# A four-layer decoder on one core: keys of the cross attentions ahead of the query, wide products of ones in every attention, and reordered slot arithmetic in the two routed layers

## The chip, the core and the metric

The kernel is one program for one core of one Trainium2 chip. The time is the device time of one execution in microseconds (us). Three runs of the kernel before took 962.3, 957.73 and 956.75 us; their median is 957.73. One further execution was recorded by the hardware profiler: it took 954.99 us, and the durations below are from it. The engines are called PE (TensorE matmuls), DVE (VectorE), ACT (ScalarE), POOL (GpSimd) and SP (SyncE, which here only issues transfers).

## The reference

The input `x` is 16 sequences of 64 tokens with 128 channels, float32, so 1024 tokens. A second input `ctx_1024` of the same shape is the context of the cross attentions. Each of four layers has an attention, a cross attention and a feed-forward part; each of the twelve is added to its input and normalised:

```python
x = _layernorm(x + _L0_attn_ref(x, ...), axis=-1)
x = _layernorm(x + _L0_xattn_ref(ctx_1024, x, ctx_1024, ...), axis=-1)
x = _layernorm(x + _L0_ffn_ref(x, ...), axis=-1)
...
x = _layernorm(x + _L3_ffn_ref(x, ...), axis=-1)
```

The cross attentions, here that of layer 1, take the query from `x`, and keys and values from the context; those of layers 0, 2 and 3 differ in masks, scale and the number of heads:

```python
q = _split_heads(Q @ Wq + bq)
k = _split_heads(K @ Wk + bk)
v = _split_heads(V @ Wv + bv)
scores = jnp.einsum('bhqd,bhkd->bhqk', q, k) / np.sqrt(HEAD_DIM)
attn = jax.nn.softmax(scores, axis=-1)
out = jnp.einsum('bhqk,bhkd->bhqd', attn, v)
...
return out @ Wo + bo
```

The feed-forward part of layer 2 sends each token to the best of 16 experts (a switch) and adds a shared expert; that of layer 3 takes the best two of 8 experts:

```python
_, top_idx = jax.lax.top_k(logits, TOP_K)          # layer 2, TOP_K = 1
...
masked_inputs = scores.T[:, :, None] * x[None, :, :]
gate_up = jnp.einsum('eth,ehf->etf', masked_inputs, gate_up_proj)
gate, up = jnp.split(gate_up, 2, axis=-1)
expert_out = jnp.einsum('etf,efh->eth', up * jax.nn.silu(gate), down_proj)
shared = jax.nn.silu(x @ w_gate.T) * (x @ w_up.T) @ w_down.T
...
topk_logits, topk_idx = jax.lax.top_k(logits, TOP_K)   # layer 3, TOP_K = 2
w = jax.nn.softmax(topk_logits, axis=-1)
...
h = jax.nn.gelu(jnp.einsum('th,ehi->tei', xt, W1) + b1, approximate=False)
y = jnp.einsum('te,teh->th', gates, jnp.einsum('tei,eih->teh', h, W2) + b2)
```

## The kernel before

**Names.** A tag stands for a sublayer: `xa0` to `xa3` are the cross attentions of layers 0 to 3, `at1` and `at3` the self attentions of layers 1 and 3, `lb` the two layers of local attention in layer 0, `sf` a feed-forward part with given experts (layer 1), `rc` the recurrence of layer 2, `sw` the switch layer (2), `tt` the top-2 layer (3).

**Two halves.** The tokens are cut into two halves of 512, h = 0 and 1. Each half is a Python generator that goes through its sublayers. `side_by_side` advances the two in turns, half 0 with a lead of 5 turns in `first_stream` (xa0, lb, at1, xa1, sf, rc, xa2, the router's scores) and of 2 in `second_stream` (at3, xa3, scores). A `yield` is thus the place where the other half's instructions are put in between. A scheduler then orders the instructions of each engine, and an engine works through its own list strictly in that order. The switch layer stands between the two streams, and the top-2 layer behind the second.

**An attention** (L400 on) first projects the query q from x (L424, L426) and then the keys: a matmul and a copy on ACT give k, and POOL multiplies it with the mask of one head group after the other to give the masked keys km (L436, four pieces of 128x512 with heads of 8 channels, eight in xa2 with heads of 4). Values v follow. Then the work goes in four steps of 64-wide blocks (eight in xa2): `weights` makes the scores in psum (L475, 16 matmuls per tile and step), takes their maximum and subtracts it on DVE (L519, L520) and the exponential on ACT (L523). `turn` transposes e on PE (L535, 2 x 4 per step) and copies it to eT on ACT (L538). `weigh` multiplies eT with the values (L556, 32 matmuls). `gather` and the projection at the end give `po`, `y` is the sum with the input, and `close` (L195 to L203) makes the statistics on DVE, the inverse deviation rstd on POOL (L198 an addition, L201 a power) and the normalised xt on DVE. `flip` transposes xt on PE (`px`) and so makes the x of the next sublayer. `steps` of the two halves alternate; the loop has a `yield` after each, and one ahead of `flip`.

**Products of ones.** `keep_busy` (L156) is a matmul of a 128x128 matrix of ones with itself, spread to 512 columns, in bf16, whose result the next matmuls into the same psum tile overwrite. It stands ahead of each projection of q and k, ahead of the unmasked scores (two per step), and, where the flag `spare` is set (L532), ahead of the transposes (two per step). `spare` is set in xa0, at3 and xa3, not in at1, xa1 and xa2. Where the scores have a mask (xa0, xa2, xa3), two matmuls of 128x512 in bf16 add it (L486).

**Relative positions.** at3 writes its relative scores to DRAM (`at_mem`) and reads them back (`at_rel`), all on SP's queue.

**The routed layers** do the expert work on 23 tiles of 128 slots. `choose` gives the one-hot choice `hots`; for the two best, weights `tt_w` come from ACT and POOL. `place` (L1192 to L1310) finds the slot of each token: `every` is the sum of the choices, `pp` the running counts on PE, `nt` the count per expert rounded up to 128, `end` and `begin` its running sums, `sf` the slot, `in_tile` and `at_row` one-hot forms of its tile and row, and `pid` a sum of 16 or 32 matmuls that gives the token of every slot; `ids` are those as integers (a free slot reads a row of zeros). `whose` and `owner` tell the expert of each tile. `tiles_in_step` gathers the rows of the tiles (`got`, on POOL's queue, six ahead), transposes them, and calls `first`, `flip` and `second` for the two layers of the expert; it also calls `between(k)` once for each tile, from k = -1.

In the switch layer the slots are gathered back at the end (`sw_back`, eight gathers on POOL's queue) and added to the shared expert's result (L1436). The shared expert of half 0 is computed at the end of half 0's stream, that of half 1 inside the switch layer: `share_up` for its two chunks f, with `between` putting the rest at tiles 0, 2 and 4.

In the top-2 layer the results are scattered to rows of `tt_out` given by `tt_outs` (on POOL's queue), and read back as `tt_back` on SP, one row of 512 bytes per partition and descriptor. The weights and the output rows of the slots come from a second sum of 16 matmuls, `tt_pw`, which the code before makes from `tt_wof` right behind `place`.

**Loads.** `load_switch_down` loads the second weights of the 16 experts ahead of the switch layer, `load_top2` (L1613) all weights of the 8 experts of the top-2 layer, 4 MB in four transfers on SP, called right behind the switch layer. `mask_zero` (L706) loads the integer mask of xa3 and turns it into additions.

Of the kernel before, what the change touches and what calls it, by code (L numbers as in the profile page):

```python
# [11 lines left out]
F32 = mybir.dt.float32  # L12
# [25 lines left out]
class Kernel:  # L38
    def __init__(self, ctx, tc, dram, where):
# [9 lines left out]
        self.xt = []  # L49
# [135 lines left out]
    def close(self, pool, h, y, tag, shift=False):  # L185
# [10 lines left out]
        for i in range(4):  # L196
            nc.vector.bn_aggr(mv[:, i, :], stats[:, i, :])  # L197
        nc.gpsimd.tensor_tensor(  # L198
            rstd, mv[:, :, 1], self.eps.to_broadcast([P, 4]), ALU.add
        )  # L200
        nc.gpsimd.tensor_tensor(rstd, rstd, self.minus.to_broadcast([P, 4]), ALU.pow)  # L201
# [43 lines left out]
    def new_y(self, tag, h):  # L245
        return self.xp.tile([P, 4, D], F32, tag=f"y{h}", name=f"y_{tag}{h}", bufs=1)
# [153 lines left out]
    def attention(  # L400
        self, h, tag, kv, hd, scale, wq, wk, wv, wo, bq=None, bk=None, bv=None, bo=None,
        mask=None, rel=None, token_mask=False, spare=False,
# [3 lines left out]
        x, kv = self.x[h], kv or self.x[h]  # L406
        work, psc, pt = self.aw, self.psc, self.pt
        per = 32 // hd
# [3 lines left out]
        if mask and tag not in self.masks:  # L412
            self.masks[tag] = mask(work)
        added = self.masks.get(tag)
        base = self.masked_base(h, bo, tag) if token_mask else self.base(h, bo, tag)
# [13 lines left out]
        def keys():  # L429

            k = project("k", wk, kv, bk)
# [63 lines left out]

        units = 4 // many
# [4 lines left out]
        km, v = keys(), values()  # L501
# [24 lines left out]
        def turn(u, gp):  # L526
            e = es.pop((u, gp))
            eT = self.buf(4, [2, HALF], f"{tag}_eT{h}{u}{gp}")
            for gg in range(2):
                ps = self.psum(pt, f"{tag}_pt{h}{u}{gp}{gg}")  # L530
                if spare:
                    self.keep_busy(ps)  # L532
# [88 lines left out]
        yield  # L621
# [84 lines left out]
    def mask_zero(self, work):  # L706

        b = work.tile([P, 8, S], BF16, tag="mask_b", name="mz_b", bufs=1)
        mi = self.buf(2, [8, S], "mz_i").bitcast(I32)
        self.nc.sync.dma_start(out=mi, in_=self.dram["mask_i"].rearrange("(a p) k -> p a k", p=P))  # L710
        self.nc.vector.tensor_scalar(b, mi, 0.0, -BIG, ALU.is_equal, ALU.mult)
        return b
# [55 lines left out]
    def local_half(self, h):  # L768
# [6 lines left out]
        for l in range(2):  # L775
# [272 lines left out]
            else:  # L1048
# [3 lines left out]
                yield  # L1052
# [4 lines left out]
    def sorted_ffn(self, h):  # L1057
        nc, x, pt = self.nc, self.x[h], self.pt
        if h == 1:
            self.close(pt, h, self.xt[h], "sf")()  # L1060
# [28 lines left out]
        yield  # L1089
# [3 lines left out]
    def recurrence(self, h):  # L1093
        nc, pt, sc = self.nc, self.pt, self.scalars
        base = self.base(h, "rc_bout", "rc")
# [27 lines left out]
        yield  # L1123
# [17 lines left out]
    def share_up(self, h, f, pool, hid, sl):  # L1141

        nc, x, gu = self.nc, self.x[h], self.g("sw_gu_s")
        pg = self.psum(pool, f"sw_pg{h}{f}")
        self.group(pg, [(gu[:, bass.ts(f, P)], x)])
# [46 lines left out]
    def place(self, tag, work, pt, hots, E, between):  # L1192
# [22 lines left out]
        over = work.tile([P, E, 8], F32, name=f"{tag}_over")  # L1215
# [673 lines left out]
```

## Time and profile before

| what | before |
|---|---|
| runs | 962.3, 957.73, 956.75 us, median 957.73 |
| profiled execution | 954.99 us, of which the span is 952.9 |
| mean granted clock of PE | 0.835 of full |
| PE matmuls | 737.7 us (77% of the span), 7005 instructions |
| PE weight loads (beside matmuls) | 473.8 us (50%) |
| DVE | 485.2 us (51%), 1103 instructions |
| ACT | 358.4 us (38%), 598 |
| POOL | 267.3 us (28%), 303 |
| chain that ended last | PE 53%, DVE 20%, POOL 9%, issue 7%, ACT 6%, DMA 4% |

The span is what the profiler saw of the program from its first to its last instruction, and the 2.1 us between it and the execution's time lie around it. Busy time of an engine is an average over stages with different limits, so the shares say which engine is fullest and not which wait decides. The granted clock is the share of full speed that the throttle gave PE. The chain is followed back from the last instruction: at each step to what released it. Where a line carries several forms of one instruction, its mean mixes them.

The sublayers stand in the span at these places (us, first scores of half 0 to where the text needs them): xa0 from 82.27, the local layers up to 385.64 (x of half 1), at1 and xa1 behind them (first scores of xa1 410.44 and 452.83), xa2's first scores 515.8 and 546.74, its last x 630.28. The switch layer's first gathered tile lands at 644.31, its last results are written from 693.1, and x of half 1 is there at 717.35. at3 begins at 719.27, xa3's scores at 793.40 and 811.22, and its last x comes at 843.76. The router's logits of the top-2 layer are there at 847.59, its first gather at 861.48, the first expert product at 867.10, and the last result at 931.67.

### The profile page before, as it was taken

The numbers are of one execution on the slowest core, as the hardware profiler recorded it, in microseconds if no ns is written. First come the engines' busy times: TensorE is split into PE (matmuls) and PEld (weight loads), VectorE is DVE, ScalarE is ACT, GpSimd is POOL, SyncE is SP. The second block draws the span as 40 slices with busy tenths as digits, with TensorE's granted clock in tenths as the row PEclk, the third lists the DMA queues.
The fourth block names the chain that finished last, engine by engine and source line by source line (L and its number), as shares of the span: only waits on it lengthen the run. The fifth ranks groups of instructions, "written<-read, shape, count | busy, mean of one in ns | idle before, by whom it ended". The sixth has DMA issues, their size and how long they took to land.

```text
span 952.9 us, 17375 instructions
## 1 busy us (share of the span) xinstructions
PE 737.7 (77%) x7005; PEld 473.8 (50%) x7006; DVE 485.2 (51%) x1103; ACT 358.4 (38%) x598; POOL 267.3 (28%) x303
## 2 busy tenths in 40 slices
PE   7767797877785998699867789968917789947990
PEld 2234456545553655357454557735603465634770
DVE  5554475655558444343445365453521484645663
ACT  2214465444543533344532344322303544502330
POOL 2332152432408011212115300017142102016732
PEclk8868899889798977668787777778968899968996
DMA  8600000000000000400000000042173430031102
GB/s 288 197 18 6 2 1 12 1 2 1 1 1 1 1 1 3 175 1 2 1 1 1 1 2 2 1 134 59 51 218 111 148 107 1 2 111 42 51 29 74
DMA packets 37078, 44.38 MB, mean 47 GB/s; under 512 B 7733, under 2 KB 29494, under 8 KB 36361
## 3 DMA queue, kind: packets, MB, share of 16 engines
q1 hardware_dynamic: 34536, 38.24, 12.8%
q0 software_dynamic: 2464, 5.05, 1.9%
q8 instruction: 56, 0.92, 0.4%
q14 instruction: 22, 0.17, 0.1%
HBM read 34.49 MB, written 11.80 MB: 49 GB/s over the span
## 4 chain that ended last, share of the span: by engine, by line
PE 53%; DVE 20%; POOL 9%; issue 7%; ACT 6%; DMA 4%; SPq 1%; DVEq 0%; POOLq 0%; ACTq 0%
PE xa_sc L475 5%; PE xa_pt L535 4%; PE xa_av L556 3%; PE tt_py L151 3%; POOL xa_km L436 3%; PE tt_ph L151 2%; PE at_pt L535 2%; DMA at_mem<-at_rsb 2%; PE xa_sc L486 2%; PE at_av L556 2%; PE lb_qk L151 2%; PE lb_pf L852 1%; DVE lb_t L816 1%; DVE lb_t L802 1%; PE sw_pe L151 1%
## 5 line engine op out<-in xcount | busy, mean ns | idle before, releaser
L519 DVE TENSOR_REDUCE xa_mx<-xa_sc 128x16 f32<-128x1024 f32 x40 | 48.8, 1220 | 99.8 <-PE xa_sc L486 65.1
L475 PE MATMUL xa_sc<-xa_km,xa_q 32*64 32x256 f32 x640 | 62.5, 452 | 18.0 <-POOL xa_km L436 12.7
L822 POOL TENSOR_TENSOR lb_t<-lb_t,lb_t 128x1024 f32<-128x1024 f32 x16 | 37.7, 2356 | 105.5 <-DVE lb_t L816 88.7
L523 ACT ACTIVATE xa_e<-xa_e 128x1024 f32<-128x1024 f32 x40 | 42.3, 1058 | 52.3 <-DVE xa_e L520 52.1
L538 ACT COPY xa_eT<-xa_pt 128x512 f32<-128x512 f32 x80 | 44.3, 588 | 44.4 <-PE xa_pt L535 44.0
L535 PE MATMUL xa_pt<-const,xa_e 128*128 128x128 f32 x320 | 52.6, 312 | 4.8 <-ACT xa_e L523 3.8
L535 PEld LDWEIGHTS xa_pt<-const,xa_e 128*128 128x128 f32 x320 | 44.0, 162 | 18.6 <-ACT xa_e L523 6.7
L520 DVE TENSOR_TENSOR xa_e<-xa_sc,xa_mx 128x1024 f32<-128x1024 f32 x40 | 48.6, 1218 | 2.4
L556 PEld LDWEIGHTS xa_av<-v,xa_eT 128*64 128x64 f32 x1280 | 43.4, 146 | 8.8 <-issue 5.8
L475 PEld LDWEIGHTS xa_sc<-xa_km,xa_q 32*64 32x64 f32 x640 | 27.1, 151 | 41.6 <-issue 19.1
L556 PE MATMUL xa_av<-v,xa_eT 128*64 128x18 f32 (+1 forms) x1280 | 47.0, 215 | 0.1
L436 POOL TENSOR_SCALAR xa_km<-xa_k,const 128x512 f32<-128x512 f32 x40 | 26.9, 691 | 55.9 <-ACT xa_k L426 45.7
L151 PE MATMUL lb_qk<-w,lb_hs 128*128 128x512 f32 x64 | 35.2, 675 | 8.7 <-DVE lb_t L816 5.2
L198 POOL TENSOR_TENSOR rstd_xa<-mv_xa,eps 128x4 f32<-128x4 f32 x8 | 1.6, 200 | 117.3 <-DVE mv_xa L197 117.3
L798 DVE TENSOR_REDUCE lb_ss<-lb_t 128x16 f32<-128x1024 f32 x16 | 19.5, 1217 | 28.4 <-ACT lb_t L795 28.4
L852 PE MATMUL lb_pf<-const,lb_t 128*128 128x128 f32 x128 | 23.7, 351 | 9.4 <-POOL lb_t L846 7.4
L156 PEld LDWEIGHTS <-ones_b 128*128 128x128 bf16 x147 | 14.9, 112 | 31.7 <-issue 16.2
L846 POOL TENSOR_TENSOR lb_t<-lb_t,lb_rs 128x1024 f32<-128x1024 f32 x16 | 30.1, 1903 | 0.0
L538 ACT COPY at_eT<-at_pt 128x512 f32<-128x512 f32 x32 | 18.0, 585 | 28.2 <-PE at_pt L535 25.5
L1552 POOL DMA_INDIRECT tt_out<-tt_ys,tt_outs x23 | 22.5, 978 | 19.5 <-DVE tt_ys L1551 16.2
L1313 POOL DMA_INDIRECT tt_got<-tt_in,tt_ids x23 | 22.3, 969 | 15.7 <-DVE tt_whose L1305 8.8
L516 DVE TENSOR_TENSOR at_rel<-at_rel,at_sc 128x1024 f32<-128x1024 f32 x8 | 9.7, 1217 | 33.2 <-PE at_sc L486 30.4
(462 smaller groups left out, 1752.6 us busy)
## 6 DMA issues: line engine op xcount, KB each, us to landing
sw_gu<-in_sw_gu SPq DMA_DIRECT2D x4, 1024.0 KB, 6.9
at_mem<-at_rsb SPq DMA_DIRECT2D x16, 256.0 KB, 2.8
at_rel<-at_mem SPq DMA_DIRECT2D x32, 128.0 KB, 2.9
w<-in_w SPq DMA_DIRECT2D x1, 3114.0 KB, 12.3
sw_dn<-in_sw_dn SPq DMA_DIRECT2D x4, 512.0 KB, 6.8
tt_w<-in_tt_w SPq DMA_DIRECT2D x2, 1024.0 KB, 8.1
tt_b<-in_tt_b SPq DMA_DIRECT2D x1, 2048.0 KB, 7.4
sw_in<-in_zeros SPq DMA_DIRECT2D x1, 1472.0 KB, 12.8
```

The source lines that it names most:

```text
L151: self.nc.tensor.matmul(out, lhsT, rhs, start=n == 0, stop=n == len(pairs) - 1)
L436: nc.gpsimd.tensor_scalar(kms[-1][:, i % 4, :], k, hm[:, i : i + 1], 1.0, ALU.mult, ALU.mult)
L475: nc.tensor.matmul(sc[64 * j : 64 * j + 64, gg, at : at + 256], q[r, t], part[r, :, t] if local else part[r, :, :], start=not masked or (p ...
L519: nc.vector.tensor_reduce(mx, scored, AX.X, ALU.max)
L520: nc.vector.tensor_tensor(e3, scored, mx.unsqueeze(2).to_broadcast([P, 16, S]), ALU.subtract)
L523: nc.scalar.activation(e3, e3, AF.Exp, scale=scale)
L535: nc.tensor.transpose(ps[:, bass.ts(n, P)], blocks[:, bass.ts(n, P)], self.g("ident"))
L538: nc.scalar.copy(eT[:, gg, :], ps)
L556: nc.tensor.matmul(av[64 * j : 64 * j + 64, pr, hp, :, :], eT[:, gg, at : at + 64], v[:, b, hp, :, :], start=True, stop=True,)
L822: nc.gpsimd.tensor_tensor(t1, t1, t2.rearrange("p t n d -> p t (n d)"), ALU.add)
L846: nc.gpsimd.tensor_tensor(t3, t3, rs[:, bass.ts(r, 16)].unsqueeze(2).to_broadcast([P, 16, 64]), ALU.mult)
L852: nc.tensor.transpose(ps[:, c, :], t1[:, t, bass.ts(c, P)], ident)
```

## The change

The change has these parts.

- **Keys ahead.** The sublayers of a half are no longer run one behind the other with `yield from`; a new `in_turn` starts the next sublayer, up to its first `yield`, when the one ahead has reached its last `yield` (marked `yield "last"`), which stands ahead of `flip`. An attention over the context makes its keys and the masked keys in this first piece; query, base and values follow in the next. Self attentions, `sf`, `rc` and `lb` have nothing in their first piece. `sorted_ffn` of half 1, which only closes, gets a `yield` of its own.
- **Ones.** `spare` is dropped, and `keep_busy` stands ahead of the transposes in all attentions: two more per step and half, that is 16 in at1 and in xa1 (four steps) and 32 in xa2 (eight steps), 64 products of 128x512 in all.
- **Switch layer.** `nt` is rounded up by adding 63.5 and a large number and taking that off again, in place of 8 comparisons and a sum. `close` of `sw` makes the inverse deviation with 11 small operations on DVE (`inverse_deviation`) in place of two on POOL. The chunk f = 1 of half 1's shared expert starts in `beside`, called inside `place` behind the 16 matmuls of `pid` in the code, with one more product of ones on `at_row`; the rest comes at tiles 0, 1 and 4. Operations of `owner` use a tile of their own.
- **Top-2 layer.** The second sum for weights and output rows (`tt_wof`, `tt_pw`) is made in `weigh`, which `tiles_in_step` calls at k = 0. It has six columns per tile in place of four: three parts of the weight, four times the row, the token's place in its group of four, and the block. Rows of `tt_out` are laid out so that `tt_back` reads four rows of 512 bytes in a piece.
- **Loads.** `load_top2` is called when half 0 of at3 has reached its last `yield`; two one-row copies on ACT, of y of at3, into the first element of every transfer's target make the transfers wait for that y. The mask of xa3 is loaded ahead of the switch layer's second weights.
- Three constants are new (`row4`, `fourth`, `block`), and the second stream has three buffers of the size of km in place of two.

```diff
+    def in_turn(self, h, *sublayers):
+        parts = [part() for part in sublayers]
+        next(parts[0])
+        for n, part in enumerate(parts):
+            if n + 1 == len(parts):
+                yield from part
+                break
+            for ahead in part:
+                if ahead == "last":
+                    next(parts[n + 1])
+                yield
...
     def attention(
...
-        def keys():
-            k = project("k", wk, kv, bk)
+        def keys(src):
+            k = project("k", wk, src, bk)
...
+        km = None
+        if kv is not None:
+            km = keys(kv)
+        yield
+        x = self.x[h]
+        kv = x if kv is None else kv
...
-        km, v = keys(), values()
+        km, v = km or keys(x), values()
...
             for gg in range(2):
                 ps = self.psum(pt, f"{tag}_pt{h}{u}{gp}{gg}")
-                if spare:
-                    self.keep_busy(ps)
+                self.keep_busy(ps)
...
         flip = self.close(pt, h, y, tag, shift=tag == "xa0")
-        yield
+        yield "last"
         flip()
...
     def sorted_ffn(self, h):
+        yield
+        x = self.x[h]
         if h == 1:
-            self.close(pt, h, self.xt[h], "sf")()
+            flip = self.close(pt, h, self.xt[h], "sf")
+            yield "last"
+            flip()
             return
...
     def close(self, pool, h, y, tag, shift=False):
...
+        if tag == "sw":
+            self.inverse_deviation(rstd, mv, self.psum(pool, f"pd_{tag}{h}"))
+        else:
...
     def share_up(self, h, f, pool, hid, sl, behind=None):
         pg = self.psum(pool, f"sw_pg{h}{f}")
+        if behind is not None:
+            nc.tensor.matmul(pg, self.ones_b, behind, start=True, stop=True)
...
     def place(self, tag, work, pt, hots, E, between, beside):
...
-        over = work.tile([P, E, 8], F32, name=f"{tag}_over")
-        nc.vector.tensor_tensor(
-            over,
-            pp[:, 8, :].unsqueeze(2).to_broadcast([P, E, 8]),
-            steps[:, 0:8].unsqueeze(1).to_broadcast([P, E, 8]),
-            ALU.is_gt,
-        )
+        large = 1.5 * 2.0**30
         nt = work.tile([P, E], F32, name=f"{tag}_nt")
-        nc.vector.tensor_reduce(nt, over, AX.X, ALU.add)
-        nc.vector.tensor_scalar(nt, nt, 128.0, None, ALU.mult)
+        nc.vector.tensor_scalar(nt, pp[:, 8, :], 63.5, large, ALU.add, ALU.add)
+        nc.vector.tensor_scalar(nt, nt, -large, None, ALU.add)
...
+        beside(at_rows)
...
-        nc.vector.tensor_tensor(free, free, pid, ALU.add)
+        row = work.tile([P, TILES * E], F32, tag=f"{tag}_row", name=f"{tag}_row")[:, :TILES]
+        nc.vector.tensor_tensor(row, free, pid, ALU.add)
         ids = work.tile([P, TILES], I32, name=f"{tag}_ids")
-        nc.vector.tensor_copy(ids, free)
+        nc.vector.tensor_copy(ids, row)
...
     def switch_ffn(self):
-            ups = [self.share_up(1, f, pt, hid1, sls[f]) for f in range(2)]
-            slot, owner, ids, _, _ = self.place("sw", one, pt, hots, E, lambda: next(ups[0]))
+            ups = [self.share_up(1, 0, pt, hid1, sls[0])]
+            def beside(at_rows):
+                ups.append(self.share_up(1, 1, pt, hid1, sls[1], at_rows[0][:, 0:4, :]))
+                next(ups[1])
+            slot, owner, ids, _, _, _ = self.place(
+                "sw", one, pt, hots, E, lambda: next(ups[0]), beside
+            )
...
             def between(k):
-                if k == 0:
-                    next(ups[0])
-                    next(ups[1])
-                elif k == 2:
-                    next(ups[1])
+                if k in (0, 1):
+                    next(ups[k])
                 elif k == 4:
                     base.append(self.share_down(1, pt, hid1))
...
     def top2_ffn(self):
...
+            def weigh(k):
+                if k != 0:
+                    return
+                of = one.tile([P, 6, 16, TILES], BF16, tag="tt_of", name="tt_wof")
...
+                nc.scalar.activation(of[:, 3, :, :], in_tile, AF.Identity, scale=self.g("row4"))
+                for n, name in ((4, "fourth"), (5, "block")):
+                    nc.vector.tensor_tensor(
+                        of[:, n, :, :],
+                        in_tile,
+                        self.g(name).unsqueeze(2).to_broadcast([P, 16, TILES]),
+                        ALU.mult,
+                    )
+                pw = pt.tile([P, 6, TILES], F32, tag="t", name="tt_pw")
...
             self.tiles_in_step(
-                "tt", work, pt, self.tt_in, ids, first, flip, second, lambda k: None
+                "tt", work, pt, self.tt_in, ids, first, flip, second, weigh
             )
...
+                    at = TILES * P + c * N + h * HALF
                     nc.sync.dma_start(
-                        out=back, in_=self.rows_of(self.tt_out, TILES * P + c * N, h)
+                        out=back,
+                        in_=self.tt_out[at : at + HALF, :].rearrange("(p a) d -> p a d", a=4),
                     )
...
-    def load_top2(self):
+    def load_top2(self, behind):
+        for t in (self.tt_w1, flat):
+            nc.scalar.copy(
+                t.rearrange("p (n m) -> p n m", m=4 * HALF)[0:1, :, 0], behind[0:1, 0, 0:2]
+            )
...
     def second_stream(self, h):
+        def third():
+            if h == 0:
+                self.load_top2(self.y_of[h])
+            yield from self.attention(
+                h, "xa3", c, 8, r8, "xa3_wq", "xa3_wk", "xa3_wv", "xa3_wo", mask=self.mask_zero
+            )
...
     def run(self, out):
         self.load("w9", "w10")
+        self.mask_i = self.late.tile([P, 8, S], I32, tag="mask_i", name="mask_i")
+        self.nc.sync.dma_start(
+            out=self.mask_i, in_=self.dram["mask_i"].rearrange("(a p) k -> p a k", p=P)
+        )
         self.load_switch_down()
         self.switch_ffn()
-        self.load_top2()
-        with self.work_pools("a3", {8: 2, 4: 8, 2: 8}):
+        with self.work_pools("a3", {8: 3, 4: 8, 2: 8}):
             self.side_by_side(self.second_stream, 2)
```

## The prediction

> **What bounds it now.** First the page's slices of the span: PE busy in tenths, and the clock it was granted.
>
> ```profile
> ## 2 busy tenths in 40 slices
> PE   7767797877785998699867789968917789947990
> ...
> PEclk8868899889798977668787777778968899968996
> ```
>
> PE is the fullest engine, but from slice 14 to 26 (333 to 640 us: at1, xa1, sf, rc, xa2) its clock is 0.6 to 0.8, against 0.9 before and after. So next the busy time by stretch (columns: stretch, us, busy us and instructions of PE, weight loads, DVE, ACT, POOL, then the clock):
>
> ```profile
> 411.00:445.00 34.00, 33.96 (x404) 24.01 (x396) 17.68 (x26) 14.50 (x21) 2.53 (x4) 0.65 0.01 2
> ...
> 512.00:555.00 43.00, 31.96 (x234) 16.85 (x234) 17.50 (x32) 10.22 (x15) 14.04 (x20) 0.69 0.00 1
> 555.00:581.00 26.00, 25.88 (x356) 18.59 (x357) 18.88 (x19) 17.07 (x26) 0.00 (x0) 0.92 0.01 2
> 581.00:613.00 32.00, 32.00 (x343) 22.91 (x339) 12.82 (x17) 11.24 (x19) 0.00 (x0) 0.63 0.01 2
> 790.00:835.00 45.00, 41.19 (x580) 28.11 (x574) 26.66 (x46) 22.91 (x37) 7.81 (x12) 1.00 0.01 2
> ```
>
> In 411 to 445 and 581 to 613 the queue is full and half cold: 12 and 11 matmuls a us. In 790 to 835 (xa3) it is warm, with 13, though that stretch holds two waits. xa0, at3 and xa3 have two wide bf16 matmuls at each step's transposes (L532, `spare`) beside two with its scores; at1, xa1 and xa2 have only the latter.
>
> Then the chain of waits (start, us, piece), at the cross attentions:
>
> ```profile
> 407.70 2.70 POOL xa_km L436 x4
> ...
> 510.42 5.34 POOL xa_km L436 x8
> ...
> 541.32 5.37 POOL xa_km L436 x8
> ...
> 790.66 2.70 POOL xa_km L436 x4
> ...
> 808.48 2.70 POOL xa_km L436 x4
> ```
>
> Scores wait for the masked keys, which depend on the context alone and yet are made after the query. Last the two routed layers, by the timeline and the DMA issues:
>
> ```profile
> 694.79 3.46 SPq L1618 DMA_DIRECT2D tt_w<-in_tt_w  x1
> ...
> 699.34 0.94 POOL L1313 DMA_INDIRECT sw_back<-sw_out,sw_slot  x1 [23.90 <-issue]
> ...
> 705.80 0.29 DVE L1436 TENSOR_TENSOR y_sw<-sw_base,sw_back 128x128 f32<-128x128 f32 x1 [12.41 <-DMA sw_back<-sw_out,sw_slot]
> ```
>
> ```profile
> sw_got<-sw_in,sw_ids POOLq DMA_INDIRECT x23, 2.5
> ...
> sw_back<-sw_out,sw_slot POOLq DMA_INDIRECT x8, 5.8
> ```
>
> The gathers that end the switch layer land in 5.8 us where like ones take 2.5: 4 MB of top-2 weights are in flight.
>
> ```profile
> 852.47 0.20 POOL L1483 TENSOR_TENSOR tt_w<-tt_ex,tt_w 128x8 f32<-128x8 f32 x1
> 852.71 0.17 DVE L1500 CAST tt_wpart<-tt_w 128x16 bf16<-128x16 f32 x1 [2.10 <-POOL tt_w L1483]
> 852.79 0.22 DVE L1203 TENSOR_TENSOR tt_every<-tt_hot 128x64 bf16<-128x64 f32 x1
> ```
>
> DVE works in order, so `tt_every`, ready at 850.6, stands 2.1 us behind a cast that waits for POOL.
>
> **The change, part by part.** Minus is time saved. Where things stand is from the built program's instruction order.
>
> *Keys ahead.* What is late next is the query: I take the gap from its copy's end to the first score. xa0 half 0: 82.27 to 79.5, but the mask's multiply (1.04) now stands behind the key masks on POOL, then 0.42 on DVE, so -2.0; half 1, where keys only change places with the query (ACT at 101.65 instead of 102.72), -1.1; together -3 (-4 to 0). xa1 half 0: scores at 410.4 now; they would wait for x_at, ready for its transposes at 388.2, at1's scores, and a query copy that ACT's order puts behind two at_eT copies, about 405: -5. xa1 half 1: 452.8 to 449.5, -3. xa2 half 0: keys can start after po_rc (501.9), eight masks are 5.4 us, and rstd's two small operations stand between them on POOL (it delays the query up to 1.3): 515.8 to 511.3, -4.5. xa2 half 1: 546.7 to 541.4, -5. These four give -17.5; the halves share PE, and what one half gains the other takes partly, so I book two thirds, -12 (-18 to -8). xa3: 793.4 to 790.3 and 811.2 to about 809, where rstd again stands between masks: -4.5 (-6 to -1).
>
> *Ones in all attentions.* 64 more matmuls of 128x512 bf16. Price: 0.21 to 0.22 us in a warm row of ones, 0.43 in a cold one (four in 1.71 at 721.6); no psum wait worth naming (xa_pt's ones idled 0.9 us in 32). What they bring: a step is 58 records, 60 with two ones. 411 to 445 are seven steps at 4.9; at xa3's 4.65, waits included, 32.6, at its 4.0 without them 28: -3.5. 581 to 613 are 5.9 steps at 5.4; at 4.1 to 4.65, 24 to 27.5: -6. 555 to 581 is warm already and only pays: +2. The rest of 340 to 555, half chain, half cold: -4. Sum -11.5, net of their price. Ends: between 330 and 634 the chain has 206 us of PE; at the warm prices (16 scores 1.05, 8 transposes 1.06, 32 weighings 1.04) I get 152, so 54 less 14 for the ones, -40; and +27 if nothing warms and all are on the path at 0.43. I stand nearer to none: the value comes from xa3's row, the same steps with the ones.
>
> That same row of 581 to 613 is full for 32 us at 0.63. [...]
>
> *One more turn of lag.* sorted_ffn gives half 1 a turn more, so xa2's last step of half 1 stands alone after half 0's close, with half 0's shared expert in its gaps: +2 (0 to +5).
>
> *Switch start.* `sw_over` and its reduce (2 x 0.3) become one small operation; between pid and ids two 0.52 operations move behind: -1.3. But the ones on at_row and pg of chunk 1 now stand after the first of 16 sw_pid matmuls: 0.4 and 1.9, +2.3 for the ids. Against it the pg and pu that held the first tile (647.8 to 651.2, so 3.4) are gone; I book -2.0 of it, for the first tile then waits for its own rows. Net -1.3 + 2.3 - 2.0 = -1 (-3 to +2.5).
>
> *Switch end.* Without the 4 MB the last write lands 2.3 us after its issue (693.8), not at 699: first gather at 696, -3.3; eighth at 704.8, lands 2.5 later. The new deviation is 11 operations of 0.2 on DVE (195.3 to 197.5 in the local layer) for 1.5 of POOL, and half 0's now wait behind half 1's four additions, thus for the eighth gather. px of half 1 about 714 instead of 717.35, and at_pq waited for that one already: -3.5 (-6 to +1).
>
> *Late top-2 weights.* Two tiny ACT copies wait for y of at3 half 0 (783.5); behind them at_att, which ran at 783.6: below 0.4. On SP the four loads (0.5, 0.8, 3.5, 0.7) stand behind all at_rel and ahead of tt_in at about 836; they landed within 10.2 us, needed at 867: nothing, and 5 if they were in the way. The zero mask's load moves ahead of sw_dn: 256 KB at 240 GB/s, 1.1 us for sw_in, hidden behind the ids. The larger constants, 17 KB: nothing.
>
> *Top-2.* `tt_every` -2.1, `tt_over` -0.3; two products of 0.53 now stand between pid and ids, +0.4; tt_pw, 138 wide, still stands ahead of the first product: -2 (-3.5 to +1). tt_back reads 2 KB rows, 3.0 to about 2.3 after issue: -0.7 (-1.2 to 0).
>
> Sum: -3 -12 -4.5 -11.5 +2 -1 -3.5 -2 -0.7 = -36.2. The profiled execution took 954.99 (span 952.9, 2.1 around it): 918.8. The median of the runs is 957.73, 2.7 above: 921.
>
> **Rivals.** *All warm*: the middle stays at full clock, the ones' term is -40: -65, 893. For it: xa3 and at3 at 1.00. Against: rc, sf and the heads of chains leave PE idle (3.7 of 10 us at 490 to 500). 0.08. *The query is as late as the keys*: small POOL operations between the masks and the other half's queue eat the gain, keys (19.5) give a third: 935. For it: xa0 half 1, where keys hardly move. 0.14. *The ones warm nothing*: a full queue is cold for another reason; in 340 to 630 they only add, 14 (warm price) to 34 (0.53, the mean of ones ahead of scores), against 24.7 of all the rest: 947 to 967, slower than before from 0.43 apiece with 58 of 64 on the path, and up to 980 if the second rival joins it (24.7 less 13). For it: xa2 has two wide mask matmuls a step and yet went cold at 581. Against: 1.00 wherever there are four a step. 0.20.
>
> **Numbers.** Forecast 0.58, mostly 905 to 935. Under 896 I leave half of all-warm (0.04), over 948 most of the third rival (0.15), together 0.19: 896 to 948. A measurement tells about 1% (948 to 967) from no change. Faster: 0.58 + 0.08 + 0.12 + 0.05 = 0.83; same 0.02 + 0.08 = 0.10; slower 0.07, the third rival's upper half.
>
> **What would show it.** Clock above 0.85 in 340 to 620 of the old time, and xa2's steps at about 4.1 us; no xa_km on the chain, or its pieces under 1 us; sw_back landing in 2.5; the first tt_got some 2 us sooner after tt_logits. It is wrong if the stretch from x_lb (385.6) to the last px_xa (630.3) shrinks by less than 10 us, or if the clock there stays below 0.8 with more PE busy.

## The result, and the profile after

Four runs of the changed kernel took 921.17 to 923.14 us, median 922.18, against a median of 957.24 of four runs of the kernel before: a ratio of 0.961 (95% interval 0.957 to 0.964). The forecast was 921. The profiled execution took 921.5 us, its span 919.7, so 33.2 less than before, where the sum of the terms was 36.2. The number was right. The terms behind it were not, as the experiments show.

First the page's slices of the span (PE busy in tenths, then the granted clock in tenths):

```profile
## 2 busy tenths in 40 slices
PE   7777878778688788889978999769557899957990
...
PEclk8766989979989897899976799879867889958995
```

In slices 16 to 25 (counted from 0, here 368 to 598 us) seven of ten read 0.8 or 0.9; before, those from 14 to 26 were at 0.6 to 0.8. Two stretches with the same beginning and end in every kernel serve from here on. M goes from the copy that makes x of half 1 behind the local layers to the last flip of xa2; Q goes from the first projection of at3 to where the top-2 router's products for half 1 begin. By the busy time in stretches (us, then busy us and instructions of PE, weight loads, DVE, ACT, POOL, then the clock), before, M and then Q:

```profile
385.64:630.28 244.64, 205.00 (x2025) 135.12 (x2025) 111.24 (x217) 96.77 (x144) 44.51 (x65) 0.76 0.05 16
719.27:845.67 126.40, 105.24 (x1328) 66.35 (x1327) 64.89 (x111) 57.36 (x85) 15.89 (x27) 0.93 0.28 86
```

and after:

```profile
384.61:594.31 209.70, 189.67 (x2081) 123.65 (x2081) 112.76 (x216) 97.64 (x144) 44.27 (x64) 0.90 0.05 17
678.72:814.74 136.02, 116.55 (x1328) 74.31 (x1327) 65.53 (x111) 57.73 (x87) 15.85 (x27) 0.85 0.36 109
```

M is 34.9 us shorter, and PE is busy 15.3 us less in it, though it has 56 records more there (56 of the 64 new products; the other 8, of half 0 in at1, lie ahead of M's start). Q is 9.6 us longer, where 4.5 of gain had been booked. The rest nearly cancels: x of the local layers is there 1.0 earlier, from the last flip of xa2 to the first projection of at3 it is 84.4 instead of 89.0 us, and from the end of Q to that of the span 105.0 instead of 107.3. All of it: -1.0 - 34.9 - 4.6 + 9.6 - 2.3 = -33.2.

The masked keys on the chain of waits after (start, us, piece):

```profile
482.27 0.70 POOL xa_km L436
482.97 0.98 POOL rstd_rc L204
483.95 4.68 POOL xa_km L436 x7
...
751.27 2.70 POOL xa_km L436 x4
...
754.21 1.05 POOL rstd_at L204
```

Those of xa1 are gone from it. Those of xa2 and xa3 are still there, but not as what the scores wait for: POOL took the masks first, and the deviation `rstd` stands behind them (the four masks of xa3 took POOL from 751.27 to 753.97, the two operations of `rstd` began at 753.93 and 754.21; the statistics were ready at 751.75).

The gathers behind the switch layer, from the DMA issues:

```profile
sw_back<-sw_out,sw_slot POOLq DMA_INDIRECT x8, 2.5
```

They land in 2.5 us, as forecast. And the head of the top-2 layer, by the timeline (the product `tt_pp` waits for `tt_every`):

```profile
819.71 0.23 DVE L1219 TENSOR_TENSOR tt_every<-tt_hot 128x64 bf16<-128x64 f32 x1
...
820.08 0.22 PE L1224 MATMUL tt_pp<-tt_every,before 128*128 128x72 bf16 x1 [3.46 <-DVE tt_every L1219]
```

`tt_every` no longer stands behind a cast: it runs 3.0 us after `tt_logits` (816.66), where it took 5.2 (847.59 to 852.79). The first gather follows `tt_logits` by 11.9 us instead of 13.9.

### The profile page after: what moved, and what is told of

Its sections match the earlier page's. It is cut to its first block, busy times and chain, and to the rows that moved or that the text cites. A ratio compares the mean times of both kernels' runs of the same rounds, so it can differ in the third digit from the quotient of the medians.

```text
span 919.7 us, 17526 instructions
## 1 busy us (share of the span) xinstructions
PE 737.2 (80%) x7069; PEld 473.0 (51%) x7071; DVE 493.5 (54%) x1126; ACT 360.2 (39%) x599; POOL 264.9 (29%) x299
## 3 DMA queue, kind: packets, MB, share of 16 engines
q1 hardware_dynamic: 33000, 38.26, 13.4%
## 4 chain that ended last, share of the span: by engine, by line
PE 57%; DVE 20%; POOL 8%; ACT 5%; issue 4%; DMA 3%; SPq 1%; DVEq 0%; POOLq 0%; ACTq 0%
PE xa_sc L475 4%; PE xa_av L566 3%; PE xa_pt L545 3%; PE tt_py L151 3%; PE sw_pe L151 3%; PE tt_ph L151 2%; PE at_pt L545 2%; POOL xa_km L436 2%; DMA at_mem<-at_rsb 2%; PE lb_qk L151 2%; PE lb_pf L860 2%; PE at_av L566 2%; PE xa_sc L486 1%; DVE lb_t L824 1%; DVE lb_t L810 1%
## 5 line engine op out<-in xcount | busy, mean ns | idle before, releaser
L475 PE MATMUL xa_sc<-xa_km,xa_q 32*64 32x256 f32 x640 | 56.4, 404 | 3.6 <-DVE xa_e L531 2.1
L545 PE MATMUL xa_pt<-const,xa_e 128*128 128x128 f32 x320 | 50.0, 286 | 2.2 <-ACT xa_e L534 2.2
L545 PEld LDWEIGHTS xa_pt<-const,xa_e 128*128 128x128 f32 x320 | 41.3, 148 | 14.4 <-ACT xa_e L534 4.5
L566 PEld LDWEIGHTS xa_av<-v,xa_eT 128*64 128x64 f32 x1280 | 40.2, 138 | 7.9 <-issue 6.2
L566 PE MATMUL xa_av<-v,xa_eT 128*64 128x18 f32 (+1 forms) x1280 | 43.7, 209 | 0.0
L156 PEld LDWEIGHTS <-ones_b 128*128 128x128 bf16 x211 | 21.4, 109 | 35.3 <-issue 21.3
L475 PEld LDWEIGHTS xa_sc<-xa_km,xa_q 32*64 32x64 f32 x640 | 25.2, 137 | 23.0 <-issue 16.1
L156 PE MATMUL xa_pt<-ones_b 128*128 128x512 bf16 x80 | 29.9, 388 | 0.0
```

The costliest lines, as they stand in the source:

```text
L156: self.nc.tensor.matmul(out, self.ones_b, self.ones_b.unsqueeze(1).to_broadcast([P, 4, P]), start=True, stop=True)
L475: nc.tensor.matmul(sc[64 * j : 64 * j + 64, gg, at : at + 256], q[r, t], part[r, :, t] if local else part[r, :, :], start=not masked or (p ...
L545: nc.tensor.transpose(ps[:, bass.ts(n, P)], blocks[:, bass.ts(n, P)], self.g("ident"))
L566: nc.tensor.matmul(av[64 * j : 64 * j + 64, pr, hp, :, :], eT[:, gg, at : at + 64], v[:, b, hp, :, :], start=True, stop=True,)
```

## The experiments

Ratios are to runs of the kernel before on the same chip. The chips differ: the kernel before has a median of 957 on the first, 959 on that of the first four experiments, 973 and 975 on those of the next two sets. What is compared between chips are stretches of the profiles. M has no transfers in its waits (the traces of before and of the change list none there, at a DMA share of 0.05), and repeats to 0.1 us wherever the instructions are the same. The routed layers do differ: from the first expert product of the top-2 layer to the end it is 84.3 to 85.8 us in the six profiles of the first two chips, and 92.5 to 95.1 in the eight of the other two.

**Without the 64 new ones.** The theory then was that the ones hold the clock and that most of M's 34.9 us is theirs.

```diff
-                self.keep_busy(ps)
+                if tag in ("xa0", "at3", "xa3"):
+                    self.keep_busy(ps)
```

> The changed kernel without its 64 new products of ones in at1, xa1 and xa2; all else as changed. Between x of the local layers and the last x of xa2 the changed kernel took 209.7 us where the kernel before took 244.6, so 34.9 less, of which I had booked 12 for the keys and 11.5 for the ones. Theory A (the ones hold PE's clock up, and that is most of it): those 34.9 shrink to about 12, so about 945 us, with the clock of that stretch near 0.76 instead of 0.89. Rival B (the keys' waits were the bound, the ones only ride along): the stretch stays near 210 or gains the price of the ones, 64 x 0.21 = 13, so 909 to 922, and the clock stays near 0.89.

Median 914.27 (911.78 to 922.21), ratio 0.966 (0.949 to 0.984; the runs of the kernel before scattered widely on this chip). M is 206.57, so shorter than with the ones, and its clock 0.87. Theory A fell, and rival B's number came.

**The ones alone**, on the kernel before.

```diff
-                if spare:
-                    self.keep_busy(ps)
+                self.keep_busy(ps)
```

> The kernel before with the 64 products of ones in at1, xa1 and xa2 and nothing else of the change. Theory A: the stretch from x of the local layers to the last x of xa2 goes from 244.6 to about 222, so about 935 us, clock of the stretch 0.85 or more. Rival B: 957 to 971, clock unchanged near 0.76. If neither part does it alone (each warms only with the other), both this and the run without new ones stay within 10 us of 957.

Ratio 0.994 (0.990 to 0.998), median 946.78. M:

```profile
381.93:613.33 231.40, 198.22 (x2081) 128.33 (x2081) 110.87 (x216) 97.61 (x144) 43.90 (x64) 0.84 0.05 15
```

Alone the ones do warm PE: the clock of M is 0.84 instead of 0.76, and M is 13.2 us shorter, against rival B, if less than the 22 of theory A. (Of the whole kernel's time the ratio gives 0.6%, about 6 of these 13 us; Q, with the instructions of before, is 135.01 us here.) So both parts raise the clock of M, and the gains do not add: with the keys ahead the ones still raise it from 0.87 to 0.90, but that no longer pays for the time they take.

**The wait in at3 filled.** In Q of the changed kernel the clock fell in a wait (windows of 1 us, columns as above):

```profile
725.00:726.00 1.00, 0.36 (x2) 0.00 (x0) 1.00 (x2) 0.00 (x0) 0.00 (x0) 1.00 0.95 314
726.00:727.00 1.00, 0.00 (x0) 0.00 (x0) 1.00 (x2) 0.04 (x1) 0.00 (x0) 1.00 1.04 350
727.00:728.00 1.00, 0.00 (x0) 0.00 (x0) 1.00 (x2) 1.00 (x1) 0.00 (x0) 0.54 1.00 281
728.00:729.00 1.00, 0.93 (x5) 0.87 (x6) 1.00 (x3) 0.01 (x1) 0.00 (x0) 0.50 0.76 189
```

```diff
-                self.keep_busy(ps)
+                for _ in range(11 if (tag, h, u, gp, gg) == ("at3", 1, 0, 0, 0) else 1):
+                    self.keep_busy(ps)
```

> The changed kernel with ten more products of ones at one place: ahead of the first transposes of half 1 in at3, where PE waited 2.7 us (725.4 to 728.1) and then ran at 0.50 until 740.6 with a full queue. Theory A (that wait set off the fall of the clock, and the fall is the larger part of the 9.6 us by which at3 and xa3 got longer): the clock stays at 1.00 there, at3 and xa3 get 5 to 7 us shorter, 916 us. Rival C (the clock falls for what is in the queue, transposes and narrow products, not for the wait): the clock still falls, and the run is 922 to 924.

Ratio 0.969 (0.957 to 0.980), median 919.0. The place itself, now full, kept its clock:

```profile
732.00:733.00 1.00, 1.00 (x6) 0.46 (x5) 1.00 (x2) 0.00 (x0) 0.00 (x0) 1.00 0.93 320
733.00:734.00 1.00, 1.00 (x6) 0.48 (x5) 1.00 (x2) 0.32 (x1) 0.00 (x0) 1.00 1.03 353
734.00:735.00 1.00, 0.71 (x5) 0.21 (x4) 1.00 (x3) 0.74 (x1) 0.00 (x0) 1.00 0.93 254
735.00:736.00 1.00, 1.00 (x10) 0.84 (x8) 1.00 (x2) 0.00 (x0) 0.00 (x0) 1.00 0.75 187
```

But it fell later, at 757.8 for 13.7 us, where PE waited 1.41 us (up to 757.02) for what follows from `rstd_at`, which stood behind the key masks of xa3 on POOL. Q was 132.8 against 136.0, within what it varies by itself (below). So the wait did set off the fall at that place, against rival C: the clock falls there in all ten other profiles of changed kernels, where PE is busy for 0.35 to 0.57 of the window with the wait. The gain in time was not seen.

**Keys of xa3 after the query.** `ahead=False` skips the early call; the keys are then made behind q.

```diff
-        if kv is not None:
+        if kv is not None and ahead:
             km = keys(kv)
...
-        km, v = km or keys(x), values()
+        km, v = km or keys(kv), values()
```

> The changed kernel, but in xa3 the keys are made after the query as before; all else as changed. Theory A: rstd of at3 half 0 no longer stands behind four key masks on POOL (it started 2.2 us after its statistics), yet the first scores wait for the masks again (3.1 us); the fall of the clock at 727.5 stays: 921 to 924. Rival D (the keys ahead are what made at3 and xa3 9.6 us longer): 912 to 914.

Ratio 0.972 (0.958 to 0.986), median 919.88, Q 133.9. That is nearer to theory A's 921 to 924 than to rival D's 912 to 914. The trace shows both sides of the exchange: `rstd` of half 0 begins 0.1 us after its statistics (748.19) instead of 2.2, and PE waits 0.60 us for the masks at the first scores of xa3. In xa3 the keys ahead neither help nor harm by an amount seen here.

**The changed kernel again.**

> The changed kernel itself, on the same chip as the next three, for their comparison and for a second profile. So far six profiles show the clock of PE as 0.50 or 1.00 only, in cells of 3.41 us on a grid that lies differently in each execution, and a cell's clock goes with how full PE was in the cell before. Theory E (what a wait costs depends on where it falls on that grid): x of the local layers, at3 and xa3 vary by several us from one execution to the next with the same instructions; at3 and xa3 (136.1 us in the first profile of the change, 126.4 in that of before) come out anywhere from 126 to 137 here, 917 to 927 in all. Rival F (the change itself makes at3 and xa3 longer): 136 again.

Ratio 0.961 (0.958 to 0.964), median 934.38: the chip is slower, the ratio the same. Q was 133.41, inside theory E's range and 2.6 below rival F's 136. M was 209.70 again: x of the local layers came at 381.1 to 392.3 us in the profiles of all runs, yet from there on the same instructions take the same time. The place on the grid is not left to chance there: M's start lay 2.28 us into a cell in the first profile of the change and 2.29 in this one. In all seven profiles with the new ones it is 2.3 to 2.4, in the seven without them 0.4 to 0.6.

**Without the new ones, beside it.**

> The changed kernel without its 64 new ones, on the same chip as the changed kernel. In the first run the stretch from x of the local layers to the last x of xa2 took 206.6 us without and 209.7 with them. Theory G (with the keys ahead, little is left to warm, and the ones cost about their price): 3 to 8 us faster than the changed kernel, the stretch 205 to 208. Rival H (the difference was the place of the grid): equal within 2 us.

Ratio 0.963 (0.960 to 0.967), against 0.961 for the changed kernel beside it. M repeats at 206.54, 3.2 us less than with the ones (theory G), but over the whole kernel the two cannot be told apart (rival H's number), so this is not a faster kernel. Rival H is not excluded for M either: with and without the ones M starts at different places of a cell, so how much of the 3.2 is the price of the ones and how much the place is open.

**Waits at sf and rc filled**, without the 64 ones.

```diff
             ps = self.psum(pool, f"px_{tag}{h}")
+            for _ in range(8 if tag in ("sf", "rc") else 0):
+                self.keep_busy(ps)
```

> As the run without the 64 new ones, but with eight products of ones ahead of each flip of sf and rc (32 in all), where PE waits for DVE's statistics and POOL's deviation; in the changed kernel PE ran at 0.50 for 33.7 of the 56 us from 471 to 527, where these flips lie. Theory E (the clock follows how full PE was in the cell before): the waits no longer drop it, cold time from 470 to 530 falls below 20 us, 4 to 10 us faster than without the ones at all. Rival B (only the waits themselves count): the ones lie in waits or on the path, so equal or up to 7 us slower (32 x 0.21).

Ratio 0.968 (0.965 to 0.972), against 0.963 (0.960 to 0.967) without these ones: not faster, and M is 210.27 instead of 206.54. The cold time there was 23.9 us from 480 to 515, against 34.1 us from 471 to 522 without them, but PE still waits 2.5 and 2.0 us at the recurrence's own products, and the ones then ran cold (eight in 3.38 us from 511.62 on, where eight at 475.71 took 1.90) or ahead of work that could have gone. Theory E's gain did not come, nor its cold time of below 20 us.

**Top-2 weights early.** The loads behind the switch layer again, without the two copies.

```diff
-        for t in (self.tt_w1, flat):
-            nc.scalar.copy(
-                t.rearrange("p (n m) -> p n m", m=4 * HALF)[0:1, :, 0], behind[0:1, 0, 0:2]
-            )
...
-            if h == 0:
-                self.load_top2(self.y_of[h])
...
         self.switch_ffn()
+        self.load_top2(None)
```

> The changed kernel with the loads of the top-2 weights right behind the switch layer again, as before, without the two copies on ACT that held them back. My term: the gathers that end the switch layer land in 5.8 instead of 2.5 us and the first one starts 5.7 to 6.2 instead of 2.9 us after the last copy of the results; from that copy to the projection of at3 22.5 us become 26 to 27, so 3.5 to 5 us slower than the changed kernel. Rival: the late loads give that back in xa3, where they now run, and the two are equal.

Ratio 0.966 (0.963 to 0.970), median 938.98, so 4.6 above the changed kernel in the same set, though the two intervals overlap. The timeline of this run (SPq is a transfer's issue on SP):

```profile
664.45 0.77 SPq L1663 DMA_DIRECT2D tt_w<-in_tt_w  x1
665.27 2.66 SPq L1659 DMA_DIRECT2D tt_w<-in_tt_w  x1
...
669.04 0.94 POOL L1323 DMA_INDIRECT sw_back<-sw_out,sw_slot  x1 [23.24 <-DMA sw_out<-sw_ys]
...
674.87 0.29 DVE L1450 TENSOR_TENSOR y_sw<-sw_base,sw_back 128x128 f32<-128x128 f32 x1 [10.99 <-DMA sw_back<-sw_out,sw_slot]
```

The first gather starts 5.5 us after the last copy of the results (663.58) instead of 2.9, and its rows are added 5.8 us later. From that copy to the projection of at3 it is 24.5 us, against 21.7 in the changed kernel beside it: the late loads are worth 2.8 by the trace. Q is 133.01 us, against 133.41 beside it, so xa3 is not seen to give them back.

**The turn, the keys, and both.** Three kernels take M apart.

*The additional turn alone*: no new ones, `ahead=False` for xa1 and xa2.

> The changed kernel without the 64 new ones and with the keys of xa1 and xa2 after the query as before; in the stretch from x of the local layers to the last x of xa2 only the additional turn of half 1 is left of the change. That stretch took 244.6 us before, 231.4 with the ones alone, 206.5 with the keys and the turn, 209.7 with all three, each the same to 0.1 us wherever the instructions of it were the same. Theory I (the keys ahead take the waits away in which PE empties, and the clock follows): 244 to 250 here. Rival J (the order of the two halves did it, through the turn): 215 or less.

Ratio 0.996 (0.991 to 1.000). M:

```profile
381.65:622.89 241.24, 201.77 (x2025) 132.74 (x2025) 110.99 (x216) 96.54 (x144) 44.51 (x65) 0.76 0.05 16
```

3.4 us shorter than before, a little below theory I's range and far from rival J's.

*No additional turn*: `sorted_ffn` of half 1 flips and goes on into the recurrence.

```diff
-            flip = self.close(pt, h, self.xt[h], "sf")
-            yield "last"
-            flip()
+            self.close(pt, h, self.xt[h], "sf")()
+            yield "on"
...
-                if ahead == "last":
+                if ahead in ("last", "on"):
                     next(parts[n + 1])
-                yield
+                if ahead != "on":
+                    yield
```

> The changed kernel without the additional turn of half 1 (sorted_ffn of half 1 closes and flips and goes on into the recurrence in the same turn, as before); keys and ones as changed. My term for the turn was +2 (0 to +5). Theory I: the stretch is 205 to 210, against 209.7. Rival J: 220 or more.

Ratio 0.964 (0.960 to 0.968), M 211.39, 1.4 above theory I's range: the turn saves 1.7 us here, where 2 of loss had been booked. Rival J's 220 did not come.

*Neither the turn nor the ones*, so the keys alone in M.

> The same without the 64 new ones: the keys ahead alone in that stretch. Theory I: 203 to 208 against 206.5 with the turn, and as fast as or faster than the changed kernel as a whole. Rival J: 215 or more.

Ratio 0.963 (0.959 to 0.968), M 210.30, two above theory I's range:

```profile
382.70:593.00 210.30, 184.14 (x2024) 121.89 (x2025) 113.34 (x216) 95.58 (x144) 45.04 (x65) 0.87 0.05 18
```

No version beat the changed kernel by an amount that its interval shows.

**The kernel before again.**

> The kernel before, for a second profile. The stretch from x of the local layers to the last x of xa2 is 244.6 again if it repeats as that of the change does. at3 and xa3 (from the first projection to the router's last product) took 126.4 us in its first profile, but 135.0 in the run with the ones alone, which has the same instructions there, and 129 to 136 in six profiles of changed kernels. If they differ from execution to execution by where transfers land, and not by the change: 128 to 136 here; if the change makes them longer: 126.

Ratio 1.000 (0.997 to 1.003). Its two stretches:

```profile
388.96:633.58 244.62, 204.99 (x2024) 135.14 (x2024) 111.22 (x217) 96.81 (x144) 44.50 (x65) 0.76 0.05 16
726.47:859.62 133.15, 110.92 (x1328) 70.78 (x1327) 64.87 (x111) 57.35 (x85) 15.89 (x27) 0.88 0.27 81
```

M repeats, Q does not: 133.15 where the first profile had 126.40. So most of the 9.6 us by which Q seemed to get longer was chance in the first pair.

M in seven of the eight combinations (the ones with the turn but without the keys were not run):

| in M | M, us | PE busy | PE not busy | clock |
|---|---|---|---|---|
| before (two profiles) | 244.6, 244.6 | 205.0 | 39.6 | 0.76 |
| turn | 241.2 | 201.8 | 39.5 | 0.76 |
| ones | 231.4 | 198.2 | 33.2 | 0.84 |
| keys | 210.3 | 184.1 | 26.2 | 0.87 |
| keys, turn (two profiles) | 206.6, 206.5 | 181.9 | 24.7 | 0.87 |
| keys, ones | 211.4 | 189.4 | 22.0 | 0.90 |
| keys, ones, turn (the change) | 209.7, 209.7 | 189.7 | 20.0 | 0.90 |

## Why the prediction was right, and where its steps failed

**Keys of xa1 and xa2: booked -12, measured -34.3** (244.6 to 210.3). This is the term that was mis-sized, by almost three. The waits themselves were counted about right: PE's time without work fell by 13.5 us, against 17.5 worked out for the four and 12 booked. The other 20.9 us are PE's busy time, with the same instructions, while the clock of M rose from 0.76 to 0.87. The prediction priced a wait at its own length, and that is the step that failed. Here the clock also fell behind a wait, from 1.00 to 0.50, and by the windows the first row that it quoted for a "full and half cold" queue, 411 to 445, is the bill for the masks of 2.70 us at 407.70 that it quoted beside it, for which PE waited 1.51 us. In windows of 3.41 us, before:

```profile
405.77:409.19 3.42, 3.16 (x48) 1.61 (x46) 0.00 (x0) 2.38 (x4) 1.49 (x3) 1.00 0.00 0
409.19:412.60 3.41, 2.16 (x26) 1.49 (x27) 1.00 (x1) 0.01 (x1) 1.20 (x2) 0.99 0.00 0
412.60:416.01 3.41, 3.37 (x38) 2.19 (x36) 3.41 (x4) 1.46 (x2) 0.00 (x0) 0.50 0.01 2
...
433.08:436.49 3.41, 3.41 (x26) 2.55 (x26) 0.00 (x0) 2.12 (x3) 0.00 (x0) 0.51 0.00 0
436.49:439.91 3.42, 3.42 (x74) 2.71 (x72) 1.52 (x2) 1.02 (x2) 0.00 (x0) 1.00 0.00 0
```

PE is busy 2.16 of 3.41 us while it waits for the masked keys, and the next seven windows, 23.9 us, are at 0.50, though PE is full. With the keys ahead and the turn, but no new ones (the second run of that kernel):

```profile
406.32:409.74 3.42, 3.36 (x59) 2.42 (x58) 3.35 (x4) 1.29 (x2) 0.00 (x0) 1.00 0.02 5
409.74:413.15 3.41, 3.41 (x40) 2.20 (x33) 3.31 (x3) 2.86 (x5) 0.00 (x0) 1.00 0.00 0
413.15:416.56 3.41, 3.41 (x58) 2.28 (x57) 3.14 (x5) 2.84 (x4) 0.05 (x1) 1.00 0.00 0
...
426.80:430.22 3.42, 3.42 (x70) 2.58 (x70) 1.69 (x9) 1.62 (x4) 1.51 (x3) 1.00 0.00 0
```

No window with a wait, no fall, and the same kind of work with no additional ones runs at 40 to 75 matmuls per window, in place of 22 to 41 in the seven cold ones.

About half of the 34.3 us is gained there: from M's start to the first flip behind xa1, the kernel with the keys alone takes 58.1 us instead of 75.4. The other half is gained between the second flip behind xa1 and the first behind xa2, 88.8 us instead of 107.3, and there the account is less simple. The second row that the prediction quoted, 581 to 613, has no wait ahead of it. In the kernel before:

```profile
576.44:579.85 3.41, 3.41 (x58) 2.56 (x56) 2.26 (x3) 2.25 (x4) 0.00 (x0) 1.00 0.00 0
579.85:583.26 3.41, 3.41 (x51) 2.19 (x51) 1.52 (x2) 2.38 (x4) 0.00 (x0) 1.00 0.02 5
583.26:586.67 3.41, 3.41 (x37) 2.96 (x35) 2.45 (x2) 1.62 (x3) 0.00 (x0) 0.50 0.00 0
```

The window ahead of the fall is full, but it holds almost nothing except scores and weighings (0.91 of it). In the second profile of before the clock falls at the same place. With the keys alone it falls twice behind full windows too (at 563.0 and 569.8), each time for one window. So the wait explains the first cold row and not the second. That the order of the products in the queue plays a part there is the author's guess; no run took that apart.

**Ones: booked -11.5, measured -13.2 alone and +1.1 (without the turn) or +3.2 (with it) behind the keys.** The size taken from xa3's row was close for the kernel before. The step that failed is the sum: two terms that feed on the same cold time were added as if they were independent. Behind the keys the ones still raise the clock (from 0.87 to 0.90) and shorten PE's time without work (by 4.2 to 4.7 us), but PE's busy time grows by 5.2 to 7.8 us.

**The turn: booked +2, measured -1.7 to -3.8.** In sum the stretch was booked at -21.5 and gave -34.9.

**xa0's keys: booked -3.** The first scores came at 79.90 instead of 82.27, about as worked out, but x of the local layers varies from 381.1 to 392.3 between executions (381.9 to 389.0 with the order of before), so nothing of it can be shown at the end.

**xa3's keys: booked -4.5.** Q is 126.4, 133.2 and 135.0 with the instructions of before, and 129.4 to 136.9, mean 133.5, in the eight profiles with those of the change: no gain shown. The rival "the query is as late as the keys" fits: the masks stand ahead of `rstd` on POOL and made it wait 2.2 us in xa3. The delay was priced for xa2 (up to 1.3), and the run with the query first shows the exchange, but Q varies by more than the 4.5.

**Switch start: booked -1, measured none.** The first expert product came 16.9 us after the router's products of half 1 began, instead of 19.2 (in the kernel before the first gathered tile was issued at 644.31 and landed at 647.03), but the last results were copied 61.0 us after them instead of 60.9. On the chip of the last set it is even 67.2 to 68.1 us in the three kernels with the change, against 64.7 in the kernel before. By the trace the first products now run at half clock (0.50 from 611.5 to 616; 2.04 and 1.91 us a pair, 1.07 and 1.02 before), where the shared expert's had run before (0.50 from 647 to 651); this was not tried by itself.

**Switch end: booked -3.5, measured -4.7** (from the last copy of the results to the projection of at3, 26.2 to 21.5). 2.8 of it are the late loads, by the run without them.

**Top-2 start and tt_back.** From the end of Q to the first expert product 20.7 instead of 21.4 us in the first pair; 22.0 and 23.3 in two other profiles with the instructions of before against 20.4 to 20.7 in the eleven with those of the change. Booked -2, and of that size. From there to the end 84.3 instead of 85.8 in the first pair, booked -0.7; but on the second chip it is 85.0 with the instructions of before and 85.1 to 85.5 with those of the change, so this gain is not shown.

So the sum held by luck, because two errors met: 13.4 us of gain were missed in M, and in Q 4.5 were booked where the first pair shows a loss of 9.6, most of it chance of that pair (a mean of 133.5 against 131.5 by all profiles). Of the signs that the prediction named, the clock (0.89 in 340 to 594), xa2's steps (3.9 us), `sw_back` and the first gather of the top-2 layer came. That of the chain did not: pieces of `xa_km` of 4.68 and 2.70 us are still on it. And the clock was read as proof of the ones, where only the run without them showed that it was not. Of the rivals, "the query is as late as the keys" fits xa3 and is false for xa1 and xa2; "the ones warm nothing" is false, but behind the keys they bring no net gain.

## What to carry to other kernels

Here a wait of 1.51 us ahead of a long run of small matmuls was followed by 23.9 us at a clock of 0.50: look at the windows behind a wait, and book both to the wait where the fall follows it. Terms that draw on the same cold time are not to be added; ask of each what is left if the other comes first. And before a stretch is explained, profile the same kernel twice: here one stretch repeated to 0.1 us and its neighbour moved by 7 to 9.

## What the runs showed of the hardware

In these profiles the clock was 0.50 or 1.00 and nothing between. In all 14 its changes lie on a grid of 3.41 us (in the first profile of before all 63 of them, in the first of the change all 57), so the falls seen in these two lasted 3.4, 6.8, 10.2, 13.7 us and so on, up to 27.3. In the first profile of before a full queue stayed at 0.50 for 23.9 us, from 412.56 on.

In these profiles a window's clock goes with what PE did in the window before it. Over their 3816 pairs of neighbouring windows, PE's busy share by its matmul records and what the clock was next (warm is 1.00, cold 0.50):

| PE busy in a window | warm, next warm too | cold, next warm |
|---|---|---|
| under 0.4 | 0 of 224 | 0 of 271 |
| 0.4 to 0.6 | 96 of 227 | 0 of 103 |
| 0.6 to 0.8 | 318 of 387 | 0 of 121 |
| 0.8 to 0.97 | 428 of 436 | 99 of 171 |
| 0.97 and more, scores and weighings under 0.4 of it | 886 of 887 | 321 of 372 |
| 0.97 and more, scores and weighings 0.4 to 0.9 | 508 of 511 | 6 of 100 |
| 0.97 and more, scores and weighings 0.9 or more | 0 of 4 | 0 of 2 |

The last two rows are what had not been expected. In full windows where scores (stationary tiles of 32 x 64) and weighings (128 x 64, up to 18 columns wide) had 0.4 to 0.9 of the time, beside other products, a warm clock stayed warm in 508 of 511, but a cold one came back in only 6 of 100. In the few windows that held hardly anything else the clock fell (4 of 4), with no wait at all; the fall at 583.2 us in the profile of before is one. This fits masks of 2.70 us, of which PE waited 1.51, with 23.9 us at half clock behind them, and ones that help there (M at 0.84 instead of 0.76). Transposes do not have that effect: there are 48 full cold windows that transposes filled by 0.8 or more, and each was followed by a warm one. The table is a count over these kernels, not an experiment on one kind of matmul by itself; what the chip counts is open.
